# Bias constants as numbers, one more add on ScalarE, and a ring of pair tiles kept in one tile with halves freed by themselves

## The chip, the cores and the metric

The kernel runs on one core of a Trainium2 chip. The metric is device time in microseconds (us) for one execution. The core's engines are TensorE (PE in the profile, its weight loads PEld), VectorE (DVE), ScalarE (ACT), GpSimd (POOL) and SyncE (SP), which here only issues DMAs. Each engine works through its own list of instructions in order, and instructions of different engines wait for each other through semaphores.

## What is computed

Two layers act on x of 4 x 1024 tokens with 256 channels, in float32. Each layer normalises, mixes tokens, adds the result to x under a gate, normalises again, and applies a feed-forward part under a second gate. The first layer's mixer is a recurrence over time, its feed-forward part a mixture of eight experts. The change lies almost wholly in the second layer, whose mixer is a pair attention:

```python
q = X @ Wq.T ; k = X @ Wk.T                      # 64 features
e = relu(sqrt(relu(q_i + k_j) + 1e-8) - sqrt(relu(-q_i - k_j) + 1e-8))   # every query i, key j, feature a
scores = einsum('bija,a->bij', e, Wphi)
ex = exp(scores - max_j(scores))
out = (ex @ V + einsum('bij,bija->bia', ex, e) @ We.T + ...) / sum_j(ex)
```

The feed-forward part of the second layer is a dense network with 1024 hidden units: two projections up, two square ones, one down, with SiLU and exact Gelu between them. `_layernorm` is (x - mean) / sqrt(var + 1e-5).

## The kernel before

`first_layer` runs first (to about 1080 us in the profile) and leaves the last 512 tokens of its own work to the second function; `pair_attention` then does the rest.

**Blocks and pairs.** `pair_attention` works in 128 blocks of 32 queries. A block has 16 half tiles of 128 x 1024: partitions are (feature group, query), columns are the 1024 keys. Two half tiles form a pair tile of 128 x 2048, so a block has 8 pairs (p = 0 to 7, halves h = 0, 1). Each pair goes through these steps:

- `begin(p)` takes a pair tile, and GpSimd adds query and key for the halves that `ADDS` gives to it ('p'): one TENSOR_SCALAR per half (L1399), then one that clips both or the one half (L1404).
- `adds(p)` lets VectorE add the halves marked 'd' (L1413). `ADDS` has one string per pair, one letter per half: 'a' ScalarE, 'p' GpSimd, 'd' VectorE.
- `pair(p)` lets ScalarE add the halves marked 'a' (Relu with the query as bias, L1424), then take the square root of the whole pair with a bias of 1e-8 (L1425), and TensorE multiply it into the block's scores (L1429).
- After the eighth pair, `top` and `exps` take the maximum (VectorE L1439, TensorE L1442, VectorE L1446) and the exponential (ScalarE L1448); `spread` copies the weights to all partitions (TensorE L1455).
- `weigh(p, h)` multiplies half h by the weights and sums (VectorE L1475, a custom instruction followed by a read of its accumulator). It is the last reader of the half.

**The order of the work** is written out by hand (`manual_schedule`: every engine's list has the order of the program). The loop goes over blocks n and pairs p; one such step is called a turn here. In turn (n, p) it emits `weigh` of half 0, the VectorE adds of the pair that is made next, `weigh` of half 1, then `work(ROOM[p])`, then it begins and makes pairs further on. It begins 14 pairs ahead of the one being weighed (`RING`), and makes (ScalarE and TensorE) two pairs behind the beginning (`LEAD`).

**The ring.** The pair tiles come from a pool of 14 buffers. `begin` asks for a new tile, which takes the buffer of the pair weighed last, and the first instruction that writes it waits until every reader and writer of the old tile is done, both weighings with them:

```python
def begin(self, p):
    self.s[p] = ring.tile([P, 2, T], F32, tag="s", name="s")
...
def weigh(self, p, h, ew):
    t = self.s[p] if h == 0 else self.s.pop(p)
```

**Work between the pairs.** `work(room)` advances generators: `tasks` (the end of four blocks: `finish`) and `stream`, in which stand the remainder of the first layer (`first_rest`), the preparation of the next batch of 1024 tokens (`prepare`), and the dense networks of 256 tokens each (`dense`, with `head` and `gate`). A `yield` with a number uses up room, a bare `yield` ends the generator's share of this turn. So a bare `yield` more moves all that follows in the stream by a turn. Dense products on TensorE are L1260, L1330 and L1351, their activations on ScalarE L1372.

**Normalisation.** `normed` computes mean and variance on VectorE (L925, L926), sqrt(var + eps) on ScalarE (L928), the reciprocal on VectorE (L930) and, for two tiles of 128 x 256 at a time, subtracts and scales on VectorE (L937), transposes on TensorE (L941), and applies the modulation on ScalarE (L944). It is called once with four tiles in `first_rest`, twice with four in each of three `prepare`, and once with two in each of sixteen `head`.

**Constants.** The three small constants under the roots lie in a tile `eps` of 128 x 3, and each activation reads its column as bias:

```python
eps = keep.tile([P, 3], F32, tag="eps", name="eps")
...
nc.scalar.activation(t, t, AF.Sqrt, bias=eps_rho)
```

Of the kernel before, what the change touches and what calls it, by code (L numbers as in the profile page):

```python
# [7 lines left out]
F32 = mybir.dt.float32  # L8
# [26 lines left out]
ADDS = ('ap', 'pp', 'pp', 'dp', 'pp', 'ap', 'dp', 'ap')  # L35
# [9 lines left out]
def block_kernel(ctx: ExitStack, tc: tile.TileContext, a, out):  # L45
# [19 lines left out]
    eps = keep.tile([P, 3], F32, tag="eps", name="eps")  # L65
    for i, v in enumerate((EPS_LN, EPS_GN, EPS_RHO)):
        nc.vector.memset(eps[:, i : i + 1], v)
# [5 lines left out]
    first_layer(tc, a, link, cols, seen, ident, eps)  # L73
    pair_attention(tc, a, link, out, cols, seen, ident, eps)
# [79 lines left out]
def first_layer(tc, a, link, cols_of, seen, ident, eps):  # L154
# [19 lines left out]
    eps_ln, eps_gn = eps[:, 0:1], eps[:, 1:2]  # L174
    cols = cols_of[0]
    with tc.tile_pool(name="fl_x", bufs=1) as xp, tc.tile_pool(name="fl_w", bufs=1) as wp, tc.tile_pool(
# [142 lines left out]
        def normed(u, first, dest, cols=cols):  # L319
# [8 lines left out]
            nc.scalar.activation(rs, mv[:, :, 1], AF.Sqrt, bias=eps_ln)  # L328
# [168 lines left out]
        def outputs(u):  # L497
# [14 lines left out]
            for cc in range(2):  # L512
                ps = misc([P, U], "var_ps")
                nc.tensor.matmul(ps, avg, sq[:, cc, :], start=True, stop=True)
                yield
                nc.scalar.activation(sq[:, cc, :], ps, AF.Sqrt, bias=eps_gn)
                del ps
# [321 lines left out]
def pair_attention(tc, a, link, out, cols_of, seen, ident, eps):  # L839
# [13 lines left out]
    eps_ln, eps_gn, eps_rho = (eps[:, i : i + 1] for i in range(3))  # L853
    src, dst = link["x1"], link["x2"]
    with tc.tile_pool(name="at_k", bufs=1) as pk, tc.tile_pool(name="at_w", bufs=1) as wp, tc.tile_pool(
        name="at_2", bufs=2
    ) as p2, tc.tile_pool(name="at_f", bufs=1) as pf, tc.tile_pool(name="at_fw", bufs=4) as pfw, tc.tile_pool(name="at_s", bufs=RING) as ring, tc.tile_pool(
# [30 lines left out]
        for i in range(2):  # L888
# [5 lines left out]
            ews.append(t)  # L894
        rows = {}
# [24 lines left out]
        def normed(xl, n, b, first, hT, cols=cols):  # L920
# [3 lines left out]
            for i in range(n):  # L924
                nc.vector.bn_stats(st[:, i, :], xl[:, i, :])  # L925
                nc.vector.bn_aggr(mv[:, i, :], st[:, i, :])  # L926
            rs = p2.tile([P, n], F32, tag="ln_rs", name="ln_rs")
            nc.scalar.activation(rs, mv[:, :, 1], AF.Sqrt, bias=eps_ln)  # L928
            yield
            nc.vector.reciprocal(rs, rs)  # L930
            for i in range(0, n, 2):
                while not banks[0]:
                    yield
                ps = bank([P, 2, 2 * P], "ln_ps")
                for j in range(2):
                    xn = p2.tile([P, C], F32, tag="ln_xn", name="ln_xn")
                    nc.vector.tensor_scalar(  # L937
                        xn, xl[:, i + j, :], mv[:, i + j, 0:1], rs[:, i + j : i + j + 1], ALU.subtract, ALU.mult
                    )
                    for cc in range(2):  # L940
                        nc.tensor.transpose(ps[:, cc, j * P : (j + 1) * P], xn[:, cc * P : (cc + 1) * P], ident)  # L941
# [802 lines left out]
```

## Time and profile before

| what | value |
|---|---|
| median of 3 runs (lowest, highest) | 4841.81 us (4838.57, 4844.68) |
| the profiled execution, its own time | 4842.18 us |
| its span | 4840.4 us |
| mean granted TensorE clock | 0.916 |
| busy: PE, DVE, ACT, POOL | 88%, 81%, 70%, 73% |
| last square root of the pair attention starts at | 4663.1 us |

The span runs from the first to the last instruction of the profiled execution. Busy shares are averages over stages: in the first layer, to about 1080 us, ScalarE and GpSimd are busy a third to a half of the time; in the pair attention all four engines are busy more than four fifths of it; after the last weighing only TensorE has much to do.

In the groups of the profile a line reads: line of the kernel, engine, operation, what is written <- what is read (partitions x elements), count | busy time in us, mean duration of one in ns | idle time of the engine just before these instructions, and who ended most of it. In the waits a line reads: who waited, <- for whom: us in total, number of times, longest. The chain that ended last is followed back from the last instruction: at each step to whatever released it, or to the instruction before it on its engine.

### The profile page before, as it was taken

To read this page: it belongs to the slowest core of one execution; us is meant where nothing else is said; L and a number is where in the kernel's file an instruction comes from. 1 tells how busy PE (TensorE), PEld (TensorE's weight loads), DVE (VectorE), ACT (ScalarE), POOL (GpSimd) and SP (SyncE) were. 2 spreads that over 40 slices of the span, in tenths; PEclk is the share of its full clock that TensorE was granted. 3 is DMA by queue.
4 is the path that set the end of the run, shared out by engine and by line. 5 is a ranking of instruction groups with operands and counts; after the bars stand their busy time and mean duration, and the time that the engine had idled before them with its cause. 6 is when DMAs were issued, how large, how long until landed. Compare 5 with 4: busy or idle time off the path is not lost.

```text
span 4840.4 us, 76605 instructions
## 1 busy us (share of the span) xinstructions
PE 4247.3 (88%) x28714; PEld 2421.3 (50%) x28714; DVE 3925.3 (81%) x6874; ACT 3411.3 (70%) x3182; POOL 3545.5 (73%) x2882
## 2 busy tenths in 40 slices
PE   6899999986889788989898989888899899898888
PEld 1233333432346455656554655555455556555567
DVE  5899999868897787888887787888877878888871
ACT  2333333228888888888987887888888888988851
POOL 3544444337898788888987888898878988989840
PEclk8799999987899898999998999999899989999899
DMA  4344333441112232312122332212132322122223
GB/s 139 91 119 118 107 111 110 129 137 34 42 62 72 78 98 73 125 56 90 64 73 84 102 110 75 89 64 77 54 112 94 106 72 90 64 75 76 77 85 116
DMA packets 255955, 429.48 MB, mean 89 GB/s; under 512 B 71784, under 2 KB 142624, under 8 KB 255328
## 3 DMA queue, kind: packets, MB, share of 16 engines
q1 hardware_dynamic: 252512, 422.09, 27.7%
q8 instruction: 226, 3.70, 0.3%
q10 hardware_dynamic: 2880, 1.98, 0.1%
q14 instruction: 145, 1.19, 0.1%
q0 software_dynamic: 192, 0.52, 0.0%
HBM read 400.32 MB, written 40.93 MB: 91 GB/s over the span
## 4 chain that ended last, share of the span: by engine, by line
PE 59%; ACT 15%; DVE 13%; issue 7%; POOL 5%; DMA 1%; SPq 0%; ACTq 0%; POOLq 0%; DVEq 0%
PE ff_ps L1330 16%; PE sc L1429 13%; ACT s L1425 7%; PE e_ps L620 7%; DVE s L1475 4%; PE ff_ps L1260 4%; PE xb L1455 3%; POOL s L1399 3%; POOL s L1404 2%; PE out_ps L1351 2%; PE o L1526 2%; DVE state L813 2%; PE proj_ps L425 2%; PE mix_ps L405 1%; ACT s L1424 1%
## 5 line engine op out<-in xcount | busy, mean ns | idle before, releaser
L1475 DVE CUSTOM_DVE_ANT_0 s<-s,xb 128x1024 f32<-128x1024 f32 x2048 | 2394.0, 1212 | 60.5 <-PE xb L1455 48.4
L1425 ACT ACTIVATE s<-s,eps 128x2048 f32<-128x2048 f32 x1024 | 2019.2, 1999 | 125.9 <-POOL s L1404 64.7
L1399 POOL TENSOR_SCALAR s<-kB,qt 128x1024 f32<-128x1024 f32 x1397 | 1599.7, 1151 | 321.7 <-DVE ew L1475 129.7
L1404 POOL TENSOR_SCALAR s<-s 128x1024 f32<-128x1024 f32 x1016 | 1427.4, 1405 | 89.1
L1429 PE MATMUL sc<-s,wsel 128*32 128x256 f32 x16384 | 1170.2, 412 | 329.4 <-ACT s L1425 328.7
L1330 PE MATMUL ff_ps<-wide,fw 128*128 128x256 f32 x4096 | 1001.8, 394 | 24.3 <-ACT wide L1372 21.1
L1429 PEld LDWEIGHTS sc<-s,wsel 128*32 128x32 f32 x16384 | 459.1, 115 | 900.1 <-ACT s L1425 482.2
L1330 PEld LDWEIGHTS ff_ps<-wide,fw 128*128 128x128 f32 x4096 | 762.5, 193 | 231.0 <-issue 102.2
L745 POOL TENSOR_TENSOR kv<-vb,out_k 128x512 f32<-128x512 f32 x256 | 323.7, 1273 | 242.9 <-DVE state L813 163.1
L1424 ACT ACTIVATE s<-kB,qt 128x1024 f32<-128x1024 f32 x387 | 439.5, 1136 | 18.2 <-DVE acc L603 17.5
L620 PE MATMUL e_ps<-wd,hid 128*128 128x512 f32 x896 | 414.6, 609 | 7.0 <-DVE acc L603 4.3
L1455 PE MATMUL xb<-ex,pick 64*128 64x256 f32 x2048 | 317.3, 432 | 46.2 <-ACT ex L1448 45.9
L813 DVE TENSOR_TENSOR_SCAN state<-dec,carry,kv 128x512 f32<-128x512 f32 x256 | 326.1, 1274 | 25.3 <-ACT dec L800 19.6
L620 PEld LDWEIGHTS e_ps<-wd,hid 128*128 128x128 f32 x896 | 169.7, 195 | 231.0 <-issue 216.9
L1413 DVE TENSOR_SCALAR s<-kB,qt 128x1024 f32<-128x1024 f32 x264 | 283.6, 1076 | 0.3 <-issue 0.3
L1455 PEld LDWEIGHTS xb<-ex,pick 64*128 64x128 f32 x2048 | 191.1, 201 | 178.9 <-ACT ex L1448 78.4
L1260 PE MATMUL ff_ps<-wide,fw 128*128 128x256 f32 x1024 | 269.9, 413 | 6.2 <-ACT wide L944 5.8
L805 ACT COPY carry<-state 128x1 f32<-128x1 f32 x255 | 47.9, 188 | 300.3 <-DVE state L813 299.8
L1439 DVE TENSOR_REDUCE sc<-sc 128x1 f32<-128x256 f32 x128 | 55.0, 430 | 243.7 <-PE sc L1429 243.6
L1314 DVE TENSOR_TENSOR wide<-ff_ps,ffn_s 128x512 f32<-128x512 f32 x128 | 87.9, 687 | 195.0 <-PE ff_ps L1330 194.6
L1260 PEld LDWEIGHTS ff_ps<-wide,fw 128*128 128x128 f32 x1024 | 200.3, 205 | 66.2 <-issue 20.6
L1448 ACT ACTIVATE ex<-sc,neg 128x256 f32<-128x256 f32 x128 | 60.7, 474 | 227.0 <-DVE neg L1446 226.3
(254 smaller groups left out, 4168.9 us busy)
## 6 DMA issues: line engine op xcount, KB each, us to landing
fw<-in_ffw_dram SPq DMA_DIRECT2D x354, 512.0 KB
vb<-vd SPq DMA_DIRECT2D x1024, 64.0 KB
lent<-vd SPq DMA_DIRECT2D x64, 514.0 KB
wd<-in_w_down_dram SPq DMA_DIRECT2D x28, 1024.0 KB
kB<-kd SPq DMA_DIRECT2D x32, 512.0 KB
lent<-in_We_dram SPq DMA_DIRECT2D x32, 512.0 KB
kd<-nd SPq DMA_DIRECT2D x24, 512.0 KB
vd<-out_v SPq DMA_DIRECT2D x8, 512.0 KB
```

The costliest lines, as they stand in the source:

```text
L620: nc.tensor.matmul(ps, hid[:, k, t * P : (t + 1) * P], wd[:, k, :], start=k == 0, stop=k == HID // P - 1)
L745: nc.gpsimd.tensor_mul(kv, vb[:, g % 2, :], ready[u]["k"][:, n // HN, :])
L813: nc.vector.tensor_tensor_scan(s[:, 1 : U + 1], dec, kv, c, ALU.mult, ALU.add)
L1260: nc.tensor.matmul(ps[:, h, :], w[:, k, o : o + P], hT[:, k, :], start=k == 0, stop=k == 1)
L1330: nc.tensor.matmul(ps[:, h, :], w[:, k * P : (k + 1) * P], of[:, k, :], start=k == 0, stop=k == 7)
L1399: nc.gpsimd.tensor_scalar(self.s[p][:, h, :], kB[self.b][i % 8], 1.0, self.query(i), ALU.mult, ALU.add)
L1404: nc.gpsimd.tensor_scalar(both, both, FLT_MAX, 0.0, ALU.min, ALU.max)
L1424: nc.scalar.activation(t[:, h, :], kB[self.b][i % 8], AF.Relu, bias=self.query(i))
L1425: nc.scalar.activation(t, t, AF.Sqrt, bias=eps_rho)
L1429: nc.tensor.matmul(self.sc[32 * j : 32 * j + 32, 0:256], wsel[:, g, 16 * (1 - s) : 16 * (1 - s) + 32], t[:, h, 256 * j : 256 * (j + 1)], s ...
L1455: nc.tensor.matmul(xb[:, 256 * j : 256 * (j + 1)], pick[q, j % 2, s, :], self.ex[q, :], start=True, stop=True)
L1475: nc.vector.tensor_tensor_reduce(t[:, h, :], t[:, h, :], self.xb[s], 1.0, 0.0, ALU.mult, ALU.add, ew[:, self.n % 4, col : col + 1])
```

## The change

It has five parts. The constants become numbers in the instruction, and the tile `eps` goes. In pair 6 half 0 moves from VectorE to ScalarE ('dp' becomes 'ap'), so that a block's 16 adds are split 11 on GpSimd, 4 on ScalarE and 1 on VectorE, from 11, 3 and 2. The ring becomes one tile with 14 places that lasts through the whole stage, with a list of free places; what a half waits for now follows from the accesses to that half alone. The tile `hid` of `first_rest` takes one of these places. In `normed` of `pair_attention` the subtract and scale goes to GpSimd, as adding the negated mean, which VectorE negates in one small instruction per call; both tiles of a pair are written first, and after two bare `yield`s the transposes follow.

```diff
@@ -32,7 +32,7 @@
 ...
-ADDS = ('ap', 'pp', 'pp', 'dp', 'pp', 'ap', 'dp', 'ap')
+ADDS = ('ap', 'pp', 'pp', 'dp', 'pp', 'ap', 'ap', 'ap')
@@ -62,16 +62,13 @@
-    eps = keep.tile([P, 3], F32, tag="eps", name="eps")
-    for i, v in enumerate((EPS_LN, EPS_GN, EPS_RHO)):
-        nc.vector.memset(eps[:, i : i + 1], v)
@@ -325,7 +321,7 @@
 ...
-            nc.scalar.activation(rs, mv[:, :, 1], AF.Sqrt, bias=eps_ln)
+            nc.scalar.activation(rs, mv[:, :, 1], AF.Sqrt, bias=EPS_LN)
@@ -513,7 +509,7 @@
 ...
-                nc.scalar.activation(sq[:, cc, :], ps, AF.Sqrt, bias=eps_gn)
+                nc.scalar.activation(sq[:, cc, :], ps, AF.Sqrt, bias=EPS_GN)
@@ -850,11 +846,10 @@
 ...
-    eps_ln, eps_gn, eps_rho = (eps[:, i : i + 1] for i in range(3))
 ...
-    ) as p2, tc.tile_pool(name="at_f", bufs=1) as pf, tc.tile_pool(name="at_fw", bufs=4) as pfw, tc.tile_pool(name="at_s", bufs=RING) as ring, tc.tile_pool(
+    ) as p2, tc.tile_pool(name="at_f", bufs=1) as pf, tc.tile_pool(name="at_fw", bufs=4) as pfw, tc.tile_pool(name="at_s", bufs=1) as ring, tc.tile_pool(
@@ -892,6 +887,8 @@
 ...
+        tiles = ring.tile([P, RING, 2, T], F32, tag="s", name="s")
+        free = list(range(RING))
@@ -924,21 +921,29 @@
 ...
                 nc.vector.bn_stats(st[:, i, :], xl[:, i, :])
                 nc.vector.bn_aggr(mv[:, i, :], st[:, i, :])
+            nc.vector.tensor_scalar_mul(mv[:, :, 0], mv[:, :, 0], -1.0)
             rs = p2.tile([P, n], F32, tag="ln_rs", name="ln_rs")
-            nc.scalar.activation(rs, mv[:, :, 1], AF.Sqrt, bias=eps_ln)
+            nc.scalar.activation(rs, mv[:, :, 1], AF.Sqrt, bias=EPS_LN)
             yield
             nc.vector.reciprocal(rs, rs)
             for i in range(0, n, 2):
+                xs = []
+                for j in range(2):
+                    xn = p2.tile([P, C], F32, tag="ln_xn", name="ln_xn")
+                    nc.gpsimd.tensor_scalar(
+                        xn, xl[:, i + j, :], mv[:, i + j, 0:1], rs[:, i + j : i + j + 1], ALU.add, ALU.mult
+                    )
+                    xs.append(xn)
+                del xn
+                yield
+                yield
                 while not banks[0]:
                     yield
                 ps = bank([P, 2, 2 * P], "ln_ps")
                 for j in range(2):
-                    xn = p2.tile([P, C], F32, tag="ln_xn", name="ln_xn")
-                    nc.vector.tensor_scalar(
-                        xn, xl[:, i + j, :], mv[:, i + j, 0:1], rs[:, i + j : i + j + 1], ALU.subtract, ALU.mult
-                    )
                     for cc in range(2):
-                        nc.tensor.transpose(ps[:, cc, j * P : (j + 1) * P], xn[:, cc * P : (cc + 1) * P], ident)
+                        nc.tensor.transpose(ps[:, cc, j * P : (j + 1) * P], xs[j][:, cc * P : (cc + 1) * P], ident)
+                del xs
                 yield
                 for cc in range(2):
@@ -1110,7 +1115,7 @@
 ...
-                nc.scalar.activation(flat[:, cc, :], ps, AF.Sqrt, bias=eps_gn)
+                nc.scalar.activation(flat[:, cc, :], ps, AF.Sqrt, bias=EPS_GN)
@@ -1156,7 +1161,8 @@
 ...
             banks[0] += 1
-            hid = ring.tile([P, 2, T], F32, tag="s", name="hid").rearrange("p h (k n) -> p (h k) n", n=U)
+            place = free.pop(0)
+            hid = tiles[:, place, :, :].rearrange("p h (k n) -> p (h k) n", n=U)
             ps = {}
@@ -1234,6 +1240,7 @@
 ...
             del last, hid, acc, gates, weighted
+            free.append(place)
             ahead[0] = RING
@@ -1388,19 +1395,22 @@
 ...

+            def tile(self, p):
+                return tiles[:, self.s[p], :, :]
+
             def query(self, i):
 ...
             def begin(self, p):
-                self.s[p] = ring.tile([P, 2, T], F32, tag="s", name="s")
+                self.s[p] = free.pop(0)
                 mine = [h for h in range(2) if self.n and self.adder(2 * p + h) == "p"]
 ...
                     nc.gpsimd.tensor_scalar(
-                        self.s[p][:, h, :], kB[self.b][i % 8], 1.0, self.query(i), ALU.mult, ALU.add
+                        self.tile(p)[:, h, :], kB[self.b][i % 8], 1.0, self.query(i), ALU.mult, ALU.add
                     )
                 if mine:
-                    both = self.s[p][:, mine[0] : mine[-1] + 1, :]
+                    both = self.tile(p)[:, mine[0] : mine[-1] + 1, :]
                     nc.gpsimd.tensor_scalar(both, both, FLT_MAX, 0.0, ALU.min, ALU.max)
@@ -1411,18 +1421,18 @@
 ...
                         nc.vector.tensor_scalar(
-                            self.s[p][:, h, :], kB[self.b][i % 8], self.query(i), 0.0, ALU.add, ALU.max
+                            self.tile(p)[:, h, :], kB[self.b][i % 8], self.query(i), 0.0, ALU.add, ALU.max
                         )
 ...
             def pair(self, p):
-                t = self.s[p]
+                t = self.tile(p)
                 s = p // 4
 ...
                         nc.scalar.activation(t[:, h, :], kB[self.b][i % 8], AF.Relu, bias=self.query(i))
-                nc.scalar.activation(t, t, AF.Sqrt, bias=eps_rho)
+                nc.scalar.activation(t, t, AF.Sqrt, bias=EPS_RHO)
                 for h in range(2):
@@ -1469,12 +1479,14 @@
 ...

             def weigh(self, p, h, ew):
-                t = self.s[p] if h == 0 else self.s.pop(p)
+                t = self.tile(p)
                 s = p // 4
                 col = 32 * s + (2 * p + h) % 8
 ...
                     t[:, h, :], t[:, h, :], self.xb[s], 1.0, 0.0, ALU.mult, ALU.add, ew[:, self.n % 4, col : col + 1]
                 )
+                if h:
+                    free.append(self.s.pop(p))

         def finish(n, ew, exT):


```

The rest of the diff takes the argument `eps` out of two signatures and their calls, and the columns of `eps` in `first_layer`.

## The prediction

> **What bounds the kernel now.** I read the busy shares first, then the chain that ended last, then the groups by line, and last the waits and the timeline of the second layer. The profiled execution took 4842.18 us, its span 4840.4; the median of the runs shown is 4841.81, so the sum below starts from 4842.
>
> ```profile
> PE 59%; ACT 15%; DVE 13%; issue 7%; POOL 5%; DMA 1%; SPq 0%; ACTq 0%; POOLq 0%; DVEq 0%
> ```
>
> TensorE carries three fifths of the chain, and four engines carry the rest. All that the change touches lies in the pair attention, from about 1080 us to its last weighing at 4663 us; what follows is dense work on TensorE. From 1300 us on this stage repeats itself: the table of busy time over one round of eight blocks (columns: stretch, its length, busy time of PE, PEld, DVE, ACT, POOL with instruction counts, granted clock, DMA share, GB/s) shows how the limits change places.
>
> ```profile
> 4278.70:4307.60 28.90, 28.90 (x246) 18.79 (x245) 21.92 (x40) 26.53 (x21) 25.28 (x22) 1.00 0.27 92
> 4337.00:4359.10 22.10, 16.68 (x124) 8.62 (x117) 21.95 (x40) 21.76 (x15) 20.58 (x17) 0.69 0.01 2
> sum 216.20, PE 191.43 PEld 119.94 DVE 183.00 ACT 190.80 POOL 193.35; mean PE 23.93 PEld 14.99 DVE 22.87 ACT 23.85 POOL 24.17
> ```
>
> In the first block TensorE is busy throughout and the others wait; in the second it has little dense work, and DVE and ACT are full. Over the round all four stand at 183 to 193 of 216 us: no engine bounds it alone, and time is lost at the changes from one limit to the other. The waits say the same:
>
> ```profile
> PE sc L1429 <- ACT s L1425: 328.7, 204, 8.1
> DVE sc L1439 <- PE sc L1429: 243.6, 79, 10.5
> ACT ex L1448 <- DVE neg L1446: 226.3, 70, 9.2
> POOL s L1399 <- DVE ew L1475: 129.7, 128, 5.1
> ```
>
> TensorE waits for square roots, VectorE for scores, ScalarE for the maximum, POOL for the weighing that frees a place. I therefore price each edit by how much of its line lies **on the chain** of this stage. Summed over its pieces from 1080 to 4663 us: L1425 347 us (some 177 square roots of 1024), L1424 69 us (65 pieces of 387 adds), L1399 and L1404 131 and 106 us, L1413 27 us (25 pieces of 264), L937 17 us, TensorE about 2140 us.
>
> **The change part by part.** The rows:
>
> ```profile
> L1425 ACT ACTIVATE s<-s,eps 128x2048 f32<-128x2048 f32 x1024 | 2019.2, 1999 | 125.9 <-POOL s L1404 64.7
> L1424 ACT ACTIVATE s<-kB,qt 128x1024 f32<-128x1024 f32 x387 | 439.5, 1136 | 18.2 <-DVE acc L603 17.5
> L1399 POOL TENSOR_SCALAR s<-kB,qt 128x1024 f32<-128x1024 f32 x1397 | 1599.7, 1151 | 321.7 <-DVE ew L1475 129.7
> L1404 POOL TENSOR_SCALAR s<-s 128x1024 f32<-128x1024 f32 x1016 | 1427.4, 1405 | 89.1
> ```
>
> ```profile
> L1372 ACT ACTIVATE wide<-wide 128x2048 f32<-128x2048 f32 x32 | 61.1, 1911 | 67.3 <-DVE wide L1314 66.9
> ```
>
> *Numbers for constants.* The square root reads its bias from the eps tile and takes 1999 ns; Gelu over the same 2048 elements reads no tile for a bias and takes 1911. The same step stands between L516 (eps, 687 ns for 512) and L567 (no bias, 598). No row shows a number other than zero as bias, so the saving lies between 0 and 92 ns; I take 92, since the difference is the same at two sizes. ScalarE sheds 1024 x 0.092 = 94 us, on the chain 177 x 0.092 = **-16**. Bounds -20 and 0.
>
> *The add moved from VectorE to ScalarE* (pair 6, 127 blocks). ScalarE gets 127 x 1.136 us; the square root behind it also waits for the add's result: in the timeline the gap between them is +0.09 us, where two square roots overlap by 0.09 us. So 1.23 us each, 156 us of work. ScalarE's net is 156 - 94 = +62 us, 0.49 per block. With the share that L1424 has on the chain now (65 of 387) 21 of the 127 end there: **+26**; all of them would be +156. VectorE loses 127 of 264 adds; half of the chain's 27 us goes: **-14**.
>
> ```profile
> L1413 DVE TENSOR_SCALAR s<-kB,qt x264: 739/964/2297, 1087.6 to 4656.2; 128x1024 f32<-128x1024 f32 x132
> L937 DVE TENSOR_SCALAR ln_xn<-wide,ln_mv,ln_rs x28: 398/1207/2022, 1168.9 to 3492.5; 128x256 f32<-128x256 f32 x28
> ```
>
> *What the two engines cost each other.* These VectorE operations (duration min/median/max) stretch up to threefold beside POOL, and POOL stretches too. Undisturbed, L1404 takes 1.041 us on one half (5 pairs x 127 = 635) and 1.894 on two (381), 1383 us in all against 1427; L1399 takes 1.122 x 1397 = 1567 against 1600. POOL loses 77 us, and 187 of the 324 VectorE operations go: 44 us. Its lines have 237 of 3027 us on the chain, 8%: **-4**. By the Trainium skill (SBUF — State Buffer, "SBUF: two separate sides") whichever of the two starts first holds the shared port pair for its whole instruction. Blocking of that kind would put 264 x 0.74 us on POOL, 195 us and not 77, and the saving would be an estimated -9; the row shows less, and the sum goes by the row.
>
> *The normalisation's subtract to POOL.* 60 operations of L937 leave VectorE (59 us busy, 17 on the chain); 23 sign changes of a few columns come, at most 0.2 us each by the smallest rows (L1441, 162 ns). On POOL each is 128x256: between a quarter of 1.122 us and the 0.73 us of L1550, the nearest row of that size; I take 0.4, 24 us, 8% of it +2. The transposes come two turns later, so they no longer wait: **-15** together. The added wait: POOL's adds queue behind a subtract that waits for VectorE's reciprocal, and ScalarE's roots wait for these adds. POOL lags VectorE nearly everywhere (1.0 us of waiting per block), so mostly nothing; in the four-tile calls the third subtract also waits for TensorE's transposes, 7 times, at most the 5.5 us by which VectorE waited for a score in the timeline, 39 us. I take **+4**, bounds 0 and 50. The Trainium skill (GPSIMD Engine Reference, "4.1 Engine selection") speaks against the step: it gives elementwise work to VectorE and calls GPSIMD roughly equal with one input tensor. By that rule the step would be worth nothing; the 1.2 us median on VectorE beside POOL says otherwise.
>
> *The ring.* The timeline of one pair with both halves on POOL:
>
> ```profile
> 4107.03 1.22 DVE L1475 CUSTOM_DVE_ANT_0 s<-s,xb 128x1024 f32<-128x1024 f32 x1
> 4108.17 0.08 DVE L1475 DVE_READ_ACCUMULATOR2_ANT ew<- 128x1 f32 x1
> 4108.45 2.22 POOL L1399 TENSOR_SCALAR s<-kB,qt 128x1024 f32<-128x1024 f32 x2 [1.99 <-PE sc L1429]
> ```
>
> POOL starts right after the second weighing (the named product merely ended at the same time). Now the first half may start 1.14 us earlier, after the first weighing. The chain enters POOL by such a pair 22 times: at most -25. Against it, the second half gets waits of its own: two adds without them overlap by 0.02 us, adds after other POOL work stand 0.09 apart. If the overlap goes, POOL pays 3 x 0.116 x 127 = 44 us, 8% of it on the chain. I take **-12**, bounds -25 and +44.
>
> *The order.* Two more turns in every normalisation push dense work back. Written out, TensorE's list behind the last score products holds 314 dense products instead of 284, each two matmul records of 0.245 us: +15 us at the end, where nothing lies beside them. The stage gets rid of the same, worth the 60% that TensorE has on the chain, -9: **+6**. The first layer loses some 0.09 us at 14 roots, mostly hidden: 0.
>
> Sum: -16 + 26 - 14 - 4 - 15 + 4 - 12 + 6 = **-25**, so 4817 us.
>
> **The rivals.** *ScalarE becomes the bound (slower).* For: it is the only engine that gains work, and in 22 of the 127 stretches from one L1446 to the next it is idle under 1.5 us. Against: on average it is idle 3.2 us per block of 27, and the net is 0.49. Break-even: the relief without its own add is 51 us, so when the added 1.23 us ends last in more than 41 of 127 blocks the kernel is slower. At 75 blocks: 92 - 51 = +41, 4883.
> *The relief is swallowed.* Where TensorE is full, faster feeders only wait longer; VectorE's and POOL's terms halve, the end stays: -16 + 26 - 7 - 2 - 8 + 4 - 6 + 6 = -3, 4839.
> *The constants cost what the tile cost, or the halves aren't freed alone* (the change doesn't do what it says): without -16 and -12 the sum is +3, 4845; it is counted with the one before.
> *More than the chain shows.* VectorE's whole 137 + 59 us and POOL's 44 us come off; if a third of TensorE's 329 us of waits for roots goes, the time is 4842 - 110 + 15 = 4747.
>
> **How the numbers follow.** A measurement here tells about 0.2%, 10 us, from no change. Chances: forecast 0.42, more 0.16, swallowed or not done 0.16, ScalarE bound 0.26. The forecast's own spread, with the bounds above, is 4790 to 4836. Faster takes nearly all of the first two cases, 0.57; same 0.14; slower the last and a little of the third, 0.29. The range runs from 4745, most of the gain, to 4895, above the slower rival since each added add that ends last costs 1.23 us.
>
> **What would show it.** L1425 near 1907 ns, x1024 (if 1999, the first term is wrong); 514 adds on ScalarE, 137 on VectorE, with a shorter median; L1404's mean nearer 1.36 us; POOL's wait for the weighing under 130 us; the last score earlier and a tail some 15 us longer. I am wrong if TensorE's wait for square roots rises above 329 us or ScalarE's share of the chain grows by several points: then the added add decides.

## The result and the profile after

Kernel before and changed kernel were timed in turns on one chip: 4839.6 us (median of 6 runs, 4835.6 to 4844.7) and 4868.5 us (4865.2 to 4876.1). The ratio is 1.0059 with a 95% interval of 1.0049 to 1.0069: the change costs 0.6%, 29 us (24 to 33). The forecast was 25 us the other way; the time lies in its range, the sign is wrong.

The groups of the changed kernel that answer to the rows of the prediction (the lines have moved by some ten: L1435 was L1425, L1434 was L1424, L1409 and L1414 were L1399 and L1404, L1423 was L1413):

```profile
L1435 ACT ACTIVATE s<-s 128x2048 f32<-128x2048 f32 x1024 | 1924.5, 1907 | 116.3 <-POOL s L1414 49.1 <-DVE s L1423 18.0 <-ACT s L1434 1.1
L1409 POOL TENSOR_SCALAR s<-kB,qt 128x1024 f32<-128x1024 f32 x1397 | 1579.5, 1136 | 326.7 <-DVE ew L1485 198.0 <-PE sc L1439 9.1 <-DVE neg L1456 8.1
L1414 POOL TENSOR_SCALAR s<-s 128x1024 f32<-128x1024 f32 x1016 | 1396.5, 1375 | 89.1
...
L1434 ACT ACTIVATE s<-kB,qt 128x1024 f32<-128x1024 f32 x514 | 585.3, 1139 | 18.5 <-DMA kB<-kd 17.8
...
L1423 DVE TENSOR_SCALAR s<-kB,qt 128x1024 f32<-128x1024 f32 x137 | 159.7, 1169 | 0.0
```

Every part does what it says, and the durations are nearly those forecast: the square root reads no tile for its bias and takes 1907 ns, 92 less; 514 adds stand on ScalarE and 137 on VectorE; GpSimd's two rows are 20 and 31 us shorter in all. Only the subtract on GpSimd is dearer, 557 ns where 0.4 us was taken. So the prices of single instructions are not what was wrong. The waits of the changed kernel show that the work did not get ahead for it:

```profile
PE sc L1439 <- ACT s L1435: 358.8, 214, 7.0
DVE sc L1449 <- PE sc L1439: 307.7, 88, 9.5
...
DVE wide L1321 <- PE ff_ps L1337: 246.7, 59, 12.2
...
ACT ex L1458 <- DVE neg L1456: 209.8, 62, 6.1
POOL s L1409 <- DVE ew L1485: 198.0, 103, 12.0
```

TensorE waits 30 us longer for square roots (329 before), although each is shorter; VectorE has 152 us less to do and waits 64 us longer for scores; GpSimd waits 198 us instead of 130 for the weighings, though a half is now free 1.14 us earlier. The longest of these waits was 5.1 us and is now 12.0: something single has been added. The prediction named the first of these as a sign that it is wrong, and expected the last to fall under 130. It also expected the last score earlier; the last square root starts at 4684.2 us, before at 4663.1. VectorE also waits 52 us longer for the dense products (195 before). The other sign that was named, ScalarE's share of the chain, can't be read here, since the chain of this profile breaks off 95 us before its end.

Where the time went shows when the stage is cut at the maxima of its blocks (columns: stretch, its length, busy time of PE, PEld, DVE, ACT, POOL with instruction counts, granted clock, DMA share, GB/s). The changed kernel from its first maximum to its eleventh, to its last, and to its end:

```profile
1112.90:1406.60 293.70, 222.95 (x1721) 103.61 (x1724) 230.50 (x432) 252.67 (x197) 228.38 (x189) 0.84 0.10 32
1406.60:4692.90 3286.30, 2904.49 (x23537) 1799.77 (x23529) 2587.82 (x4770) 2856.00 (x2184) 2804.55 (x2322) 0.92 0.26 83
4692.90:4863.40 170.50, 149.44 (x666) 127.11 (x665) 41.36 (x78) 18.29 (x19) 4.34 (x5) 0.95 0.38 125
```

Before, the three stretches take 288.2, 3283.2 and 165.0 us (shown below). So 5.5 us are lost in the first ten blocks, 3.1 in the other 117 and 5.5 behind the last maximum. Another 8.9 lie ahead of the first maximum, 7.1 of them between VectorE's first add and that maximum. The sum is 23 us and not 29, as the profiled execution of the changed kernel is the fastest of its six.

### The profile page after: what moved, and what is told of

The parts are those of the page before. It is cut to its first block, busy times and chain, and to the rows that moved or that the text cites. A ratio compares the mean times of both kernels' runs of the same rounds, so it can differ in the third digit from the quotient of the medians.

```text
span 4863.4 us, 76805 instructions
## 1 busy us (share of the span) xinstructions
PE 4262.4 (88%) x28714; PEld 2424.6 (50%) x28714; DVE 3773.1 (78%) x6707; ACT 3455.0 (71%) x3310; POOL 3527.0 (73%) x2942
## 5 line engine op out<-in xcount | busy, mean ns | idle before, releaser
L1435 ACT ACTIVATE s<-s 128x2048 f32<-128x2048 f32 x1024 | 1924.5, 1907 | 116.3 <-POOL s L1414 49.1
L1409 POOL TENSOR_SCALAR s<-kB,qt 128x1024 f32<-128x1024 f32 x1397 | 1579.5, 1136 | 326.7 <-DVE ew L1485 198.0
L1439 PE MATMUL sc<-s,wsel 128*32 128x256 f32 x16384 | 1182.6, 414 | 360.0 <-ACT s L1435 358.8
L1414 POOL TENSOR_SCALAR s<-s 128x1024 f32<-128x1024 f32 x1016 | 1396.5, 1375 | 89.1
L1337 PE MATMUL ff_ps<-wide,fw 128*128 128x256 f32 x4096 | 991.5, 391 | 25.7 <-ACT wide L1379 24.2
L1434 ACT ACTIVATE s<-kB,qt 128x1024 f32<-128x1024 f32 x514 | 585.3, 1139 | 18.5 <-DMA kB<-kd 17.8
L1267 PE MATMUL ff_ps<-wide,fw 128*128 128x256 f32 x1024 | 265.9, 409 | 12.3 <-DMA fw<-in_ffw_dram 11.6
L811 DVE TENSOR_TENSOR pr<-state,rec 128x512 f32<-128x512 f32 x256 | 176.0, 688 | 37.6 <-ACT state L807 9.6
```

The lines of the kernel that those rows point to most:

```text
L1267: nc.tensor.matmul(ps[:, h, :], w[:, k, o : o + P], hT[:, k, :], start=k == 0, stop=k == 1)
L1337: nc.tensor.matmul(ps[:, h, :], w[:, k * P : (k + 1) * P], of[:, k, :], start=k == 0, stop=k == 7)
L1409: nc.gpsimd.tensor_scalar(self.tile(p)[:, h, :], kB[self.b][i % 8], 1.0, self.query(i), ALU.mult, ALU.add)
L1414: nc.gpsimd.tensor_scalar(both, both, FLT_MAX, 0.0, ALU.min, ALU.max)
L1434: nc.scalar.activation(t[:, h, :], kB[self.b][i % 8], AF.Relu, bias=self.query(i))
L1435: nc.scalar.activation(t, t, AF.Sqrt, bias=EPS_RHO)
```

## The experiments

Three theories stood against each other at first. **ORDER**: the two bare yields in the normalisation push dense work back, and that costs more than 6 us. **SCALARE**: the added add ends last far more often than in 21 of 127 blocks. **RING**: the ring as one tile costs time instead of gaining 12 us. Below, a cost in us is the measured ratio to the kernel before, timed in turns with it, less one, times 4840; the brackets are its 95% interval.

### One part alone

Four kernels are the kernel before with one part of the change each, by the lines of the change shown above. The edits in short:

```diff
y1_const:
-                nc.scalar.activation(t, t, AF.Sqrt, bias=eps_rho)
+                nc.scalar.activation(t, t, AF.Sqrt, bias=EPS_RHO)
y2_add:
-ADDS = ('ap', 'pp', 'pp', 'dp', 'pp', 'ap', 'dp', 'ap')
+ADDS = ('ap', 'pp', 'pp', 'dp', 'pp', 'ap', 'ap', 'ap')
y3_ring:
-                self.s[p] = ring.tile([P, 2, T], F32, tag="s", name="s")
+                self.s[p] = free.pop(0)
y4_ln:
-                    nc.vector.tensor_scalar(
+                    nc.gpsimd.tensor_scalar(
...
+                yield
+                yield
```

> The kernel before with the constants as numbers alone. 1024 roots at 1907 instead of 1999 ns. By the forecast's term 16 us faster, 4824; bounds 0 (if the roots lie beside other work) to 94 us faster (if ScalarE were the bound). All three theories agree on faster or same; ORDER and SCALARE expect 4810 to 4830.

> The kernel before with one group of adds in each block moved from VectorE to ScalarE alone, roots still at 1999 ns. By the forecast's terms 26 lost on ScalarE and 14 gained on VectorE, so 12 slower, 4852. Theory SCALARE: 60 to 120 us slower (128 x 1.14 = 146 us on an engine that then leads). Theory ORDER: the forecast's 4852 or less.

> The kernel before with the ring of pair tiles as one lasting tile alone, each half freed by its own weighing. Forecast's term: 12 us faster, 4828. Theory RING: 15 to 35 slower, 4855 to 4875, with GpSimd's wait for the weighing up from 130 to 190 us or more. ORDER and SCALARE: 4820 to 4842.

> The kernel before with the LayerNorm edit alone (subtract on GpSimd, two added yields in each normalised tile). Theory ORDER: 20 to 45 slower, 4860 to 4885, with the swings of the dense work and the longer tail of the changed kernel (314 products, 361 weight loads). SCALARE and RING: 4835 to 4845 or, by the forecast's terms (subtract and waits -11 together with the turns +6), 4835.

Measured: constants **-23** (-29 to -17), add **+41** (35 to 48), ring **+13** (7 to 17), normalisation **+16** (10 to 22). The terms of the forecast were -16, +8 (26 - 14 - 4), -12 and -5 (-15 + 4 + 6). Two terms are right in sign, though the add costs five times its term, and two are wrong in sign. All three theories hold a part of the loss, and each part is smaller than its theory had it (60 to 120, 15 to 35, 20 to 45). RING's mark, GpSimd's wait for the weighing, is 197 us with the ring alone.

### One part undone

Four kernels are the changed kernel with one part as it was before:

```diff
x1_ln_back:
-                    nc.gpsimd.tensor_scalar(
+                    nc.vector.tensor_scalar(
...
-                yield
-                yield
x2_add_back:
-ADDS = ('ap', 'pp', 'pp', 'dp', 'pp', 'ap', 'ap', 'ap')
+ADDS = ('ap', 'pp', 'pp', 'dp', 'pp', 'ap', 'dp', 'ap')
x3_ring_back:
-                self.s[p] = free.pop(0)
+                self.s[p] = ring.tile([P, 2, T], F32, tag="s", name="s")
x4_eps_back:
-                nc.scalar.activation(t, t, AF.Sqrt, bias=EPS_RHO)
+                nc.scalar.activation(t, t, AF.Sqrt, bias=eps_rho)
```

> The changed kernel with the LayerNorm's subtract back on VectorE and without the two added yields (constants, adds 11/4/1 and the ring tile stay); the order of the dense products is then that of the kernel before (284 dense products behind the last block of attention, against 314, and 354 loads of FFN weights against 361). Theory ORDER (the two bare yields displace dense work, swings grow, weights are loaded again, the tail is longer): falls from 4868 to below the kernel before, 4810 to 4830, tail after the last maximum from 159 to about 154. Theory SCALARE (the 128 added adds of 1.14 us cost more than the 92 ns saved on 1024 roots): stays at 4865 or rises by up to 15, since VectorE gets back 60 subtracts. Theory RING (the lasting tile makes GpSimd wait longer for the weighing): stays at 4865 to 4880.

> The changed kernel with the adds split as before (VectorE keeps its share, ScalarE has a group less in each block; constants, LayerNorm edit and ring tile stay). Theory ORDER: stays above the kernel before, 4855 to 4875 (the order with 314 products in the tail stays). Theory SCALARE: ScalarE loses 128 x 1.14 = 146 us of work and the time falls by 30 to 60, to 4810 to 4840; the waits of the score matmul for the root's tile fall from 359 to under 300 us. Theory RING: 4855 to 4875, GpSimd's wait for the weighing stays near 198 us.

> The changed kernel with the ring of pair tiles in a pool as before, a tile freed as a whole (constants, adds 11/4/1 and the LayerNorm edit stay). Theory RING: falls by 20 to 35 to 4835 to 4850, and GpSimd's wait of its add for the weighing falls from 198 to about 130 us. Theories ORDER and SCALARE: does not fall; by the term of the forecast (12 us gained by halves) it rises to 4870 to 4890.

> The changed kernel with the constants as tiles again (a pointer each, as before). All theories: slower, since each root takes 1999 ns instead of 1907 ns, 94 us of ScalarE in all. By the forecast's term 16 us, so 4880 to 4890; if ScalarE bounds the kernel after the change, nearly all of it, 4930 to 4960. So the rise by this kernel is a measure of how far ScalarE is the bound: 16 is a sixth, 94 the whole.

Against the kernel before they stand at +1 (-3 to 6), +4 (0 to 8), +18 (12 to 24) and +61 (54 to 68) us, and the changed kernel at +29. So undoing the normalisation gains 27 us, undoing the add 25, undoing the ring 11, and undoing the constants costs 32, a third of the 94 us. No theory explains the loss alone: x1_ln_back, x2_add_back and x3_ring_back came out at 4842, 4845 and 4859 us, each above what its theory expected, and the wait for square roots fell to 345 us without the add, not under 300. The constants are worth more beside the other parts than alone (32 against 23), the add costs less beside them (25 against 41): both act on ScalarE, and together they do not simply add up (tested below).

### The normalisation: turns or engine

```diff
z3_ln_pool (y4_ln without the yields):
-                yield
-                yield
z4_ln_turns (y4_ln with the subtract on VectorE):
-                    nc.gpsimd.tensor_scalar(
+                    nc.vector.tensor_scalar(
```

> The kernel before with the LayerNorm's subtract on GpSimd, but no added yields: the order of TensorE, ScalarE and the DMA queue is that of the kernel before (tail of 284 products). Theory ORDER (the turns cost, not the engine): 4830 to 4842, against 4855 with the turns. Theory POOL (60 subtracts of 0.56 us on GpSimd, in front of which it waits for VectorE's reciprocal, cost): 4850 to 4870, more than with the turns, since the transposes now wait for GpSimd at once.

> The kernel before with the two added yields alone, the subtract stays on VectorE. Theory ORDER: 4855 to 4862, all of the cost of the LayerNorm edit, with the tail of 314 products 5 to 8 us longer and the swings of the stage as in the whole edit. Theory POOL: 4838 to 4848, by the tail alone at most 4848.

Measured: the subtract on GpSimd alone 0 (-3 to 5), the two turns alone **+16** (11 to 22). ORDER holds for this part, and GpSimd is neither gain nor loss. The stretch behind the last block's maximum shows what the forecast called the tail (columns as above), first in the kernel before, then with the turns alone:

```profile
4675.40:4840.40 165.00, 136.42 (x604) 115.76 (x602) 40.55 (x77) 18.50 (x19) 3.25 (x3) 0.93 0.35 117
```

```profile
4683.90:4856.40 172.50, 151.64 (x667) 128.77 (x666) 41.90 (x79) 18.38 (x19) 3.25 (x3) 0.94 0.36 124
```

TensorE has 15.2 us more to do there, as forecast, but the stretch grows by 7.5 us only: TensorE was idle for 28.6 us of it and is now for 20.9. Work was lying beside the added products after all. The six profiles with the turns have 170.5 to 172.5 us there, all others 164.8 to 168.4. Of the rest, 4.2 us lie ahead of the first maximum, where all kernels scatter, and 4.3 between the first maximum and the last. The forecast gave the stage 9 us back for the products that leave it; it gave none.

That the stage loses through unevenness is not shown. The kernel with the turns takes 6.3 us longer for the first ten blocks, in which neither kernel has a dense product, and 2.0 less for the other 117, with swings: counted from the first maximum it is 22 us ahead of the kernel before at the 29th block and 11 behind at the 53rd. How uneven TensorE's list has become depends on where a block is cut. From one block's last score product to the next, 24 blocks of the kernel before hold over 30 dense products and 9 blocks after the 13th under 12, with the turns 33 and 20; cut at the products that find the maximum, the numbers are 23 and 20, with the turns 24 and 22. Also, 361 loads of dense weights are issued instead of 354.

### The ring: early start or halves

The trace of y3_ring shows where the 12 us wait comes from. GpSimd at the start of the second layer, in the kernel before and then with the ring alone (columns: start, duration, engine, line, operation, out<-in, and in brackets the idle time before it):

```profile
1084.00 0.73 POOL L608 TENSOR_TENSOR x<-x,acc 128x256 f32<-128x256 f32 x1 [1.69 <-DVE acc L607]
...
1087.43 0.71 POOL L608 TENSOR_TENSOR x<-x,acc 128x256 f32<-128x256 f32 x1 [1.84 <-DVE acc L607]
...
1089.58 1.13 POOL L1399 TENSOR_SCALAR s<-kB,qt 128x1024 f32<-128x1024 f32 x1
```

```profile
1078.24 1.12 POOL L1406 TENSOR_SCALAR s<-kB,qt 128x1024 f32<-128x1024 f32 x1 [7.61 <-issue]
1079.44 1.04 POOL L1411 TENSOR_SCALAR s<-s 128x1024 f32<-128x1024 f32 x1
1084.48 0.72 POOL L608 TENSOR_TENSOR x<-x,acc 128x256 f32<-128x256 f32 x1 [3.99 <-DVE acc L607]
1085.30 1.12 POOL L1406 TENSOR_SCALAR s<-kB,qt 128x1024 f32<-128x1024 f32 x1
...
1122.35 1.12 POOL L1406 TENSOR_SCALAR s<-kB,qt 128x1024 f32<-128x1024 f32 x1 [12.11 <-DVE ew L1482]
```

With the pool, GpSimd ends its work on the first layer (`x`, L608) before most of its adds for the second block. With the one lasting tile, eleven adds and clips stand ahead of the last `x` instead of one, and they run beside VectorE's adds for the first block. Apart from that, GpSimd's list is the same in both kernels from first to last. Having run ahead, GpSimd then waits 12 us for the first weighing. VectorE in the same stretch, before and then with the ring alone:

```profile
1087.64 1.72 DVE L1413 TENSOR_SCALAR s<-kB,qt 128x1024 f32<-128x1024 f32 x2 [0.30 <-issue]
...
1092.55 7.05 DVE L1413 TENSOR_SCALAR s<-kB,qt 128x1024 f32<-128x1024 f32 x6
```

```profile
1091.56 3.79 DVE L1420 TENSOR_SCALAR s<-kB,qt 128x1024 f32<-128x1024 f32 x2 [0.29 <-issue]
...
1100.60 8.75 DVE L1420 TENSOR_SCALAR s<-kB,qt 128x1024 f32<-128x1024 f32 x6
```

VectorE's adds are what the first block waits for, and they stretch beside GpSimd: two take 3.79 us instead of 1.72, six 8.75 instead of 7.05, and all ten of the block 16.5 instead of 11.5. The first block's maximum comes 16.4 us after VectorE's first add in the kernel before, and 23.3 after it with the ring alone. In all five kernels with this order (the changed one, x1_ln_back, x2_add_back, x4_eps_back and y3_ring) that distance is 6.9 to 7.2 us longer than before, in none of the others more than 1.3. Two kernels take the early start away. One takes each place from the pool when it is first needed, which gives GpSimd the order of before, and frees halves alone as the change does; the other one lets GpSimd add the second half first, so that its first add waits for the second weighing as with a whole tile:

```diff
z2_ring_place (y3_ring with):
-        tiles = ring.tile([P, RING, 2, T], F32, tag="s", name="s")
+        tiles = {}
...
+        def taken():
+            k = free.pop(0)
+            if k not in tiles:
+                tiles[k] = ring.tile([P, 2, T], F32, tag="s", name="s")
+            return k
z7_second_first (z2_ring_place with):
-                for h in mine:
+                for h in reversed(mine):
```

> The kernel before with halves freed one by one and the list of free places, but each place taken from the pool of 14 when it is first needed, and then kept. GpSimd's list then has the order of the kernel before at the start of the second layer; with the one lasting tile, its first adds stand ahead of the last work of the first layer and begin 12 us earlier, beside VectorE's adds of the first block, and the first maximum came 7 us later than the stage began. Theory START (that collision is the whole cost of the ring): 4839 to 4846, against 4852 with the one tile, and the first maximum as in the kernel before; by the stage's own gain after that (some 4 us) even 4835. Theory HALVES (the second half's own waits cost): stays at 4848 to 4856.

> The kernel z2_ring_place with GpSimd adding the second half of a pair before the first, where it adds both (381 pairs). The first add then waits for the second weighing, as with the whole tile, and the other add's own wait has long been met. If the early start beside the second weighing costs what is left of the ring (8 us), 4839 to 4842; if the added waits cost it, 4846 to 4852; if the early start brought a gain that something else swallows, above 4852.

Measured: +7 (3 to 11) and +1 (-2 to 6). The time of z2_ring_place does not decide by itself: its median, 4848.8 us, is at the lower end of what HALVES expected, and by the ratio it is 4847, between the two ranges. But its first maximum is back to 16.6 us after the first add, so the early start is shown; it is worth some 6 us of the ring's 13 by the ratios and 6.9 by the distance. From the first maximum to the last z2_ring_place takes 0.3 us less than the kernel before and z7_second_first 0.3 more: freed by halves or as a whole, the stage runs the same. GpSimd's waits say why:

```profile
POOL s L1413 <- DVE ew L1489: 178.8, 146, 6.2
```

It starts its first half earlier and then stands before the second weighing, which ends when it always did: 179 us of waiting in z2_ring_place, against 129.7 in the kernel before and 129.4 in z7_second_first. The wait has moved by one instruction. The +7 that is left of z2_ring_place lies outside the stage in its profile: 3 us before it, where all kernels scatter (the last scan of the first layer's recurrence ends 3.0 us earlier to 5.8 later than in the kernel before, with no order by edits), and 3 us in the tail, at a granted clock of 0.91 instead of 0.93; y1_const, which has the ring of before, shows the same 168.2 us and 0.91 there. z7_second_first lies 6 us lower, which by its expectation would lay the 7 to the early first halves; but the two take the same time for the stage. Whether the edit makes the 7 us, the runs do not settle; beside the constants they came back in one pair of kernels at most (below).

### The add: its own cost and the relief

z2_ring_place with VectorE's add of pair 6 cut to 8 of 1024 columns measures the relief of VectorE and GpSimd without an add on ScalarE:

```diff
z5_cut (z2_ring_place with):
+                        w = 8 if self.n > 1 and p == 6 else T
                         nc.vector.tensor_scalar(
-                            self.tile(p)[:, h, :], kB[self.b][i % 8], self.query(i), 0.0, ALU.add, ALU.max
+                            self.tile(p)[:, h, 0:w], kB[self.b][i % 8][:, 0:w], self.query(i), 0.0, ALU.add, ALU.max
```

> The kernel z2_ring_place with VectorE's add of pair 6 cut to 8 of its 1024 columns from the third block on (126 adds; the rest of that half then holds old numbers): the relief of VectorE and GpSimd without ScalarE's added add. By the forecast's terms 14 and 4, so 18 us under z2_ring_place. Theory SCALARE (its added add carries the loss of 41 us, the relief is as forecast): 15 to 25 under it, so that the add itself costs 55 to 65. Theory NO RELIEF (VectorE's adds lie beside other work): within 5 us of z2_ring_place, and ScalarE's add costs 36 to 46, about 33 of 127 at 1.23 us.

Measured: 0 (-4 to 4) against the kernel before, so 7 us under z2_ring_place by the ratios, 10 by the medians, 13 from the first to the last maximum of the profiles. The 13 is one execution, the fastest of its eleven and 9 us under their median, so it is the least certain. The relief is about half of the 18 forecast, between the ranges of the two theories. The added add then costs 41 + 7, about **48 us**, 39 of 127 blocks at 1.23 us and not 21; by the profiles alone, 33 us of growth from the first maximum to the last and 13 of relief, it is 46. With the intervals of the ratios it can be some 39 to 57. The chain of y2_add shows the sign that the prediction had named, with ScalarE at 20% of it instead of 15%:

```profile
PE 57%; ACT 20%; DVE 9%; issue 7%; POOL 4%; DMA 2%; SPq 1%; ACTq 0%; POOLq 0%; DVEq 0%
```

Where the added add costs, the traces of the kernel before and of y2_add tell; each cut at its own first, eleventh and last maximum:

```profile
1104.00:1392.20 288.20, 223.81 (x1732) 105.12 (x1732) 250.03 (x448) 248.28 (x186) 240.20 (x193) 0.86 0.11 35
1392.20:4675.40 3283.20, 2906.70 (x23580) 1808.44 (x23581) 2727.11 (x4917) 2812.38 (x2066) 2823.20 (x2268) 0.92 0.25 82
```

```profile
1104.10:1405.40 301.30, 230.24 (x1733) 107.78 (x1732) 239.48 (x438) 258.81 (x196) 237.09 (x195) 0.83 0.10 32
1405.40:4708.20 3302.80, 2925.75 (x23587) 1815.72 (x23580) 2618.15 (x4800) 2939.22 (x2184) 2780.41 (x2266) 0.92 0.24 82
```

The first ten blocks grow by 13.1 us, 1.3 us each: here there is no dense work of the second layer, and the growth is as if every added add ended last. The other 117 blocks grow by 19.6 us, 0.17 each. A mean share of the whole stage mixed the two. The constants alone show the same split: their first ten blocks are 5 us shorter, two thirds of what the roots in them save, the others 26.0 us, or 0.22 of 0.74 each. In the first ten, TensorE's busy time also grows by 6.4 us with the same instructions, at a clock of 0.83 instead of 0.86.

### Constants with one part each, and the change mended

```diff
w1_const_place: y1_const with z2_ring_place
w2_const_add:   y1_const with y2_add
w3_const_pool:  y1_const with z3_ln_pool
v1_mended:      the change without the added yields, places taken as in z2_ring_place
v2_no_add:      v1_mended with the adds split as before
```

> Constants as numbers together with halves freed one by one in places taken from the pool (the ring of z2_ring_place). If the ring's remaining 7 us are of its own making, 4819 to 4826, above the constants alone (4816); if they are scatter, 4812 to 4817; if halves help once the roots are shorter, under 4810.

> Constants as numbers together with the adds split 11/4/1, no other part. Theory SCALARE: the add's cost falls from 41 us since ScalarE has been given 94 us; by the change with and without the add (4868 against 4845) it is 23, so 4836 to 4842; if the two merely add up (-23 and +41), 4858.

> Constants as numbers together with the LayerNorm's subtract on GpSimd and no added yields. The subtract alone was worth nothing, so 4812 to 4820; if VectorE's relief counts once the roots are shorter, 4800 to 4810.

> The whole change mended in the two places found: no added yields in the normalisation, and the places of the ring taken one at a time from the pool (order of the kernel before at the stage's start). If the causes found are the whole loss and add up on constants with add (4838), 4826 to 4840; if others are left, above 4845.

> The same, and the adds split as before: constants, GpSimd's subtract without yields, places from the pool with halves freed alone. With halves worth nothing it is the constants with the subtract, 4803 to 4812; if the halves help once the rest is shorter, under 4800; if they cost 7 as alone, 4813 to 4818.

Measured against the kernel before: w1_const_place -26 (-32 to -20), w2_const_add -5 (-10 to -1), w3_const_pool **-35** (-41 to -29), v1_mended -4 (-8 to 0), v2_no_add -29 (-36 to -23).

Constants and add do not merely add up: -23 and +41 would be +18, and it is -5; the 94 us that the roots give back are partly what the add uses. Halves freed alone gain nothing beside the constants either: -26 against -23 with the constants, and -29 against -35 with the subtract on GpSimd as well; the intervals overlap. The subtract on GpSimd, worth nothing alone, gains 12 us beside the constants and 3 when the places are added, so a gain is not shown for certain.

Mending the two faults of order brings the change from +29 to -4, 33 us; taking the add back brings 25 more. Alone the two faults cost 16 and 6, 22 in all. The difference lies in the stage: from the first maximum to the last the changed kernel takes 17 us longer than v1_mended, and x2_add_back 21 longer than v2_no_add, where the turns alone add 4. So the turns cost more beside the other parts; in which wait is not shown. These three causes carry the loss, and the best kernels here are w3_const_pool, 4807.6 us, and v2_no_add, 4810.0.

## Why the prediction was wrong

**The constants (-16): right in mechanism and price, the size too small.** The root went from 1999 to 1907 ns, as forecast. The 1024 roots save 94 us, of which 23 arrived alone and 32 beside the other parts: 24% to 34% of them, against the 17% that the chain of waits gave. The Trainium skill ("ScalarE: Activation LUTs", "What ACT_TABLE_LOAD costs") puts a bias read through a pointer at about 93 ns more than a number; the trace has 92.

**The add (+26) is a step that failed.** "With the share that L1424 has on the chain now (65 of 387) 21 of the 127 end there": this let the new add be like a mean add of the kernel. It isn't. In ten blocks each one cost its full time, and its cost was about 48 us in all; the relief (-14 and -4) came to about -7. The first rival, ScalarE as the bound, named the right place, but its condition, more than 41 of 127 blocks, was not shown to be reached: the cost is that of about 39 blocks with the add alone, and of fewer in the whole change, where the add came to +25 net, since the constants lightened ScalarE. The kernel was slower all the same, because the gains that the rival set against the add were not there.

**The normalisation (-15 and +4) is a step that failed:** 17 us of the subtract lay on the chain, but taking it from VectorE gained nothing, so something else must have been as late; z3_ln_pool is the kernel before to within 5 us. A subtract on GpSimd took 557 ns and not 0.4 us, 33 us in all and not 24. The waits that were feared on GpSimd cost nothing that these runs can tell.

**The order (+6) is a step that failed:** the two turns cost 16 us alone, and undoing the normalisation gained 27. The +15 at the end came to 7.5, as TensorE had idle time there; the -9 in the stage did not come, and the stage lost 4 alone and some 20 beside the other parts, which the forecast did not price at all. In which wait these lie is not shown.

**The ring (-12) is a step that failed twice.** The gain of the halves was nil: a pair's clip needs both halves, so the earlier start of the first became a wait before the second. And its cost was looked for in waits alone; that GpSimd's list changes at the start of the stage was not looked at, as only TensorE's list was written out. That cost some 6 us.

**The contention (-4)** is in GpSimd's rows (20 and 31 us less busy, 44 forecast) and perhaps in the relief of z5_cut; alone it can't be told. One reading there was too low: L937 went from 398 to 2022 ns, fivefold and not threefold.

The terms summed to -25. Alone the parts sum to +47, and together they give +29: the constants and the add make up for 23 between them. That the time lies in the stated range is owed to the range's width.

## What to carry to other kernels

A share of the chain taken over a long stage is no price for one added instruction: look at the blocks one by one for those in which the engine has no slack, and count these. Before pricing a change to buffers or yields, write out every engine's list in both kernels and read where the first difference stands, at the edges of a stage above all. Freeing the first half of what an engine needs as a whole only moved its wait here, and a part that gains nothing alone may be worth trying again after the bound has shifted.

## What the runs showed of the hardware

The granted clock made small delays larger. In the stretch without dense work the same group of 16 score products took 1.07 us at a granted clock of 1.00, after a short gap, and 1.94 at 0.50, after a long one, in the kernel before:

```profile
1158.66 1.07 PE L1429 MATMUL sc<-s,wsel 128*32 128x256 f32 x16 [0.69 <-ACT s L1425]
1166.19 1.94 PE L1429 MATMUL sc<-s,wsel 128*32 128x256 f32 x16 [6.45 <-ACT s L1425]
...
1178.42 1.93 PE L1429 MATMUL sc<-s,wsel 128*32 128x256 f32 x16 [2.29 <-ACT s L1425]
```

Over the first ten blocks the same products (1732 and 1733) took 214.1 us at a clock of 0.89 with the constants alone, 223.8 at 0.86 before, and 230.2 at 0.83 with the add alone. So in these kernels a feeder that was late also slowed the engine that it feeds. The Trainium skill ("TensorE: Matmul & The Clock Gate", "What's actually happening") says that the clock falls to half after an idle window of about 3.4 us; the third line has 1.93 us, at 0.50, after a wait of only 2.29. In this trace the clock fell at 1161.0 and at 1178.1, and the 3.41 us before each held TensorE work (columns as above):

```profile
1157.62:1161.03 3.41, 1.42 (x24) 0.42 (x16) 3.38 (x10) 0.99 (x1) 3.31 (x3) 1.00 0.00 0
1174.68:1178.10 3.42, 1.46 (x12) 0.82 (x10) 3.42 (x6) 3.39 (x3) 3.30 (x3) 1.00 0.00 0
```

So such a stretch need not be wholly idle. From the first maximum to the last, the clock of this kernel fell 80 times; TensorE was busy for 0% to 63% of the 3.41 us before each fall, and for 84% or more of the 3.41 us before each rise.

VectorE's adds of the first block show how far GpSimd can slow VectorE: beside its adds a pair of them took 3.79 us, without them 1.72.
